# Seven edge tiles of a graph kernel are placed and scattered ahead of the count of all edges

## The chip, the cores and the metric

The kernel runs on one core of one Trainium2 chip. The metric is the time of one execution on the device, in microseconds; the median of three executions of the kernel before is 2573.27 us (2565.25 to 2579.46).

## What is computed

A graph layer with a mixture block and a mixture of experts behind it. There are 3125 nodes with 512 values each and 50000 edges. Cut to what matters here:

```python
edge_dst, edge_src = edge_index[0], edge_index[1]       # "src" and "dst" of the inputs
w   = ssp(edge_attr @ W_f1) @ W_f2 * (ssp(s0 @ W_s1) @ W_s2)
out0 = w1 * x0e * sh0[:, None] + w4 * einsum('eum,em->eu', x1e, sh1) / sqrt(3)
out1 = ...                                               # x0e, x1e are rows x[edge_src]
out  = segment_sum(concat(out0, out1), edge_dst, num_segments=N)
x = x + gnn(layernorm(x), ...) + linear_attention(layernorm(x))
x = x + mixture_of_experts(layernorm(x))
```

The edges arrive sorted by the inputs' `dst`, but the sum runs over the other index, so the kernel sorts the edges itself.

## The kernel before, in words

**Stage 1, up to about 565 us.** The 50000 edges form 391 tiles of 128 edges, in 14 chunks of 28 tiles (`CT = 28`; `ST = 7` tiles make a segment, `GC = 4` segments a chunk). An edge has a record of 48 floats (`rec`): four values of `edge_attr_4` (loaded as `sh`), both node numbers, the place of its node in its group, and 32 hidden values (`ssp` of `edge_attr_32 @ W_f1`). Nodes fall into 25 groups of 125, and each group into two halves, so there are `NU = 50` lists. A list has `PER * P = 1024` fixed slots (`ROOM`); what does not fit goes to overflow tiles. To find the slot of an edge, the kernel needs its rank in its list:

- `hot(c)` (L252): for each chunk a one-hot table of the edges' lists, 128 x 1400 in bf16, built by VectorE; fourteen of them.
- The count of all edges: 56 matmuls (L260), four per chunk, add the tables up per segment into `ps_tot`; VectorE reduces them (`sums`, L267), two small matmuls make the edges before each segment (`ps_c`) and the totals (`ps_n`), and some twenty VectorE steps (L289 to L313) make `starts` out of them.
- `earlier(c)` (L327, L329) makes `seen`, the edges of the tiles before within the segment; `ranked(c, ks)` (L339, L340, L343) adds three matmuls per segment: the edges above in the tile, `seen`, and `starts`. `own_ranks` (L351) picks each edge's rank, `places` (L358 to L375) turns it into the row of `recs`, held in `at_i`. The last instruction of each call of `places` is noted in `found`.
- `spread` (L419, TensorE), `softened` (L427 to L429, ScalarE), `begin` (L403 to L408) and `joined` (L438, VectorE) fill the record; chunks 0 and 1 stay in SBUF, the others are stored in DRAM (`lined`, L446) and fetched again (`recall`, L519).
- `place(n, behind)` (L529) issues the next `n` scatters on GpSimd: one indirect DMA for each tile, from its records to the rows `recs[at_i]`. With `behind` a scatter also waits for a TensorE instruction, so that they are spread over the stage.

Chunk 0 is counted and placed first, on its own. Then `place(12)` and a hand-ordered schedule of turns follow, in which the chunks 1 to 13 and the 25 node tiles (layer norm, turning, keys) are interleaved; two calls `place(3, last)` stand in each turn. Then a loop over node columns (`place(3, last)` and single ones) and a loop over the 25 node tiles that makes the gather tables `rows_d` and `rows_s` (two calls of `place(2, last)` and one of `place(1, last)` per tile, L987, L1002 and L1025 are the matmuls they wait for). `place(2 * T)` issues what is left. A scatter waits for the clearing of the fixed slots (`cleared`, L183), too.

**Stage 2** loads the sorted records `rec<-recs` (L1104), once all scatters have landed, and then gathers rows, weighs and sums them; **stage 3** is the mixture of experts. Neither is touched by the change.

The order of instructions outside the hand-ordered parts is set by the program's order and by `tc.issue_after`, which puts an instruction behind another in its engine's queue. Each engine runs its queue in order. SP's and ACT's queues also issue loads: SP has `to_i`, `of_i`, `w_f`, `ea` and `sh` of chunks 0 and 1, `random_matrix` and the first three `x`; ACT has `b_out`, `W_o0`, `W_o1` and `W_kT` (1 MB), of which `by_random` (L493) makes `r_W_kT` with 32 matmuls before the first turn.

Of the kernel before, what the change touches and what calls it, by code (L numbers as in the profile page):

```python
# [17 lines left out]
P = 128  # L18
EDGES = 50000
TG = 125  # L20
# [31 lines left out]
def gnn_mix_moe_kernel(ctx: ExitStack, tc: tile.TileContext, a: dict, out: bass.AP):  # L52
# [90 lines left out]
    with ExitStack() as c1:  # L143
# [24 lines left out]

        w_f1 = tmp.tile([P, 4, HID], F32, name="w_f1")
# [77 lines left out]
        hots, counts = [], []  # L247
        ps_t = psum.tile([P, ST * NU], F32, name="ps_tot", tag="at")[:NSG]
        for c in range(NC):
            ts = slice(c * CT, (c + 1) * CT)  # L250
            hots.append(
                nc.vector.tensor_tensor(  # L252
                    hot(c).rearrange("p g (i b) -> p g i b", b=NU),
                    in_half_b[:, ts].rearrange("p (g i) -> p g i", i=ST).unsqueeze(3).to_broadcast([P, GC, ST, NU]),
                    lane_b.unsqueeze(1).unsqueeze(1).to_broadcast([P, GC, ST, NU]), op=ALU.is_equal,
                )
            )
            for g in range(c * GC, (c + 1) * GC):
                counts.append(
                    nc.tensor.matmul(  # L260
                        ps_t, only[:, NSG - 1 - g : 2 * NSG - 1 - g],
                        hot(c)[:, g - c * GC, :],
                        start=(g == 0), stop=(g == NSG - 1),
                    )
                )
        sums = tmp.tile([P, NU], F32, name="sums")
        nc.vector.tensor_reduce(sums[:NSG], ps_t.rearrange("g (i b) -> g b i", b=NU), AX.X, ALU.add)  # L267
        ps_c = psum.tile([P, NU], F32, name="ps_c", tag="t", bufs=1)
        nc.tensor.matmul(ps_c, before2[:NSG, :], sums[:NSG], start=True, stop=True)
        ps_n = psum.tile([P, NU], F32, name="ps_n", tag="k", bufs=1)  # L270
        nc.tensor.matmul(ps_n, ones[:NSG, :], sums[:NSG], start=True, stop=True)


        side_i = tmp.tile([P, T], I32, name="side_i")
        nc.vector.tensor_single_scalar(side_i, in_half_i, 1, op=ALU.bitwise_and)
        in_half = tmp.tile([P, T], F32, name="in_half")
        with tc.issue_after(hots[-1].ins):
            nc.vector.tensor_copy(in_half, in_half_i)
        local = tmp.tile([P, T], F32, name="local")
        nc.vector.scalar_tensor_tensor(local, in_half, -TG / 2, to_i, op0=ALU.mult, op1=ALU.add)  # L280
        nc.vector.scalar_tensor_tensor(local, side_i, -0.5, local, op0=ALU.mult, op1=ALU.add)
        far = float((NFIX + OF) * P - ROOM)
        base_ = tmp.tile([P, T], F32, name="base_")
        nc.vector.scalar_tensor_tensor(base_, side_i, -1.0, in_half, op0=ALU.mult, op1=ALU.add)
        nc.vector.tensor_scalar(base_, base_, float(ROOM // 2), far, op0=ALU.mult, op1=ALU.subtract)


        held = srt.tile([P, NG, 2], F32, name="held")
        nc.vector.tensor_copy(held.rearrange("p b h -> p (b h)"), ps_n)  # L289
        many_i = tmp.tile([P, NG, 2], I32, name="many_i")  # L290
        nc.vector.tensor_scalar(many_i, held, float(P - 1 - ROOM), 0.0, op0=ALU.add, op1=ALU.max)
        nc.vector.tensor_single_scalar(many_i, many_i, 7, op=ALU.arith_shift_right)
        many = tmp.tile([P, NG, 2], F32, name="many")
        nc.vector.tensor_copy(many, many_i)
        first = srt.tile([P, 2, NG], F32, name="first")
        for k in range(2):
            nc.vector.tensor_tensor_scan(
                first[:, k, :], ones[:, :NG], many[:, :, k], 0.0, op0=ALU.mult, op1=ALU.add
            )
        nc.vector.tensor_max(pairs_used, first[:, 0, NG - 1 :], first[:, 1, NG - 1 :])  # L300
        nc.vector.tensor_sub(first, first, many.rearrange("p b h -> p h b"))
        over_at = tmp.tile([P, NG, 2], F32, name="over_at")
        nc.vector.tensor_scalar(
            over_at, first.rearrange("p h b -> p b h"), float(-OF), 65536.0, op0=ALU.add, op1=ALU.mult
        )
        base_i = tmp.tile([P, NU], I32, name="base_i")
        nc.vector.tensor_copy(base_i, ps_c)
        nc.vector.tensor_single_scalar(base_i[:LO], base_i[:LO], -256, op=ALU.bitwise_and)
        nc.vector.tensor_single_scalar(base_i[LO:], base_i[LO:], 255, op=ALU.bitwise_and)
        starts = tmp.tile([P, NU], BF16, name="starts")  # L310
        nc.vector.tensor_copy(starts[:LO].rearrange("p (b h) -> p b h", h=2), over_at[:LO])
        nc.vector.tensor_copy(starts[:NSG], base_i[:NSG])
        nc.vector.tensor_copy(starts[LO:], base_i[LO:])  # L313
# [19 lines left out]
        def ranked(c, ks):  # L333

            so = seen[c % 2]
            for k in ks:
                g = c * GC + k
                ps = ranks[k] = psum.tile([P, ST * NU], F32, name="ps_at", tag="at")
                nc.tensor.matmul(ps, after_b, hot(c)[:, k, :], start=True, stop=False)  # L339
                nc.tensor.matmul(  # L340
                    ps[:, NU:], ones_b, so[:, k, 1:, :].rearrange("p i b -> p (i b)"), start=False, stop=False
                )
                nc.tensor.matmul(  # L343
                    ps.rearrange("p (i b) -> p i b", b=NU), part_of[:, g : g + 1].to_broadcast([P, P]),
                    starts.unsqueeze(1).to_broadcast([P, ST, NU]), start=False, stop=True,
                )

        def own_ranks(c, ks):

            for k in ks:  # L350
                nc.vector.tensor_mul(  # L351
                    mine[:, k * ST : (k + 1) * ST, :].rearrange("p i b -> p (i b)"), ranks.pop(k), hot(c)[:, k, :]
                )

        def places(c):

            ts = slice(c * CT, (c + 1) * CT)
            nc.vector.tensor_reduce(slot, mine, AX.X, ALU.add)  # L358
            nc.vector.tensor_copy(slot_i, slot)


            nc.vector.tensor_single_scalar(rank, slot_i, 65535, op=ALU.bitwise_and)
            nc.vector.tensor_single_scalar(which, slot_i, 16, op=ALU.arith_shift_right)
            nc.vector.scalar_tensor_tensor(moved, which, float(P), base_[:, ts], op0=ALU.mult, op1=ALU.subtract)
            nc.vector.scalar_tensor_tensor(moved, rank, float(ROOM), moved, op0=ALU.is_ge, op1=ALU.mult)
            nc.vector.scalar_tensor_tensor(moved, moved, far, base_[:, ts], op0=ALU.add, op1=ALU.add)
            nc.vector.tensor_add(slot_i, moved, rank)

            at = at_i[:, ts]
            nc.vector.tensor_scalar(at, slot_i, P - 1, 2, op0=ALU.bitwise_and, op1=ALU.logical_shift_left)  # L370
            nc.vector.tensor_scalar(which, slot_i, 6, 2, op0=ALU.arith_shift_right, op1=ALU.bitwise_and)
            nc.vector.tensor_tensor(at, at, which, op=ALU.bitwise_or)
            nc.vector.tensor_scalar(which, slot_i, -2 * P, 1, op0=ALU.bitwise_and, op1=ALU.logical_shift_left)
            nc.vector.tensor_tensor(at, at, which, op=ALU.bitwise_or)
# [9 lines left out]
        def edges_of(c):  # L384
# [3 lines left out]
            nc.sync.dma_start(  # L388
                ea, a["edge_attr"][:, c * CT * P : (c + 1) * CT * P].rearrange("f (r e) -> r f e", r=4)
            )  # L390
            sh = mk.tile([P, CT, 4], F32, name="sh")
# [30 lines left out]
        def softened(c, part):  # L422
# [6 lines left out]
            nc.scalar.activation(sp[:, :m], sp[:, :m], AF.Ln, bias=half, scale=0.5)  # L429
            sps[c, part] = ps, sp  # L430

        def joined(c, part):

            ps, sp = sps.pop((c, part))
            i0, i1 = PARTS[part]
            m = i1 - i0
            for r in range(4):
# [9 lines left out]

        edges_of(0)
        edges_of(1)
        with tc.issue_after(hots[-1].ins):  # L450
            begin(0)
        with tc.issue_after(counts[len(counts) // 2].ins):
            for part in range(2):
                spread(0, part)
                softened(0, part)
        earlier(0)
        for ks in ((0, 1), (2, 3)):
            ranked(0, ks)
            own_ranks(0, ks)
        places(0)  # L460
        for part in range(2):
            joined(0, part)
# [3 lines left out]
        def load(name, shape, src, pool=w, tag=None):  # L466
            t_ = pool.tile(shape, F32, name=name, tag=tag or name)
            nc.scalar.dma_start(t_, src)
# [31 lines left out]
        w_rk = by_random("W_kT", wide("W_kT"))  # L500
# [15 lines left out]
        def recall(c):  # L516
            if DIRECT <= c < T // CT:
                again[c] = chk.tile([P, CT, REC], F32, name="again", bufs=2)
                nc.gpsimd.dma_start(again[c], lined[c])  # L519

# [1418 lines left out]
```

## Time and profile before

| what | value |
|---|---|
| median of three executions | 2573.27 us |
| profiled execution | 2575.68 us |
| its span | 2573.9 us |
| PE / DVE / ACT / POOL busy in the span | 91% / 64% / 49% / 59% |
| first to last scatter, L529 | 46.24 to 565.13 us, 391 of them |
| stage 2 and 3 | 565 to 2574 us |

PE is TensorE, PEld its weight loads, DVE is VectorE, ACT is ScalarE, POOL is GpSimd and SP is SyncE; a letter q behind an engine's name marks its queue. A line of the timeline has start, duration, engine, line of the kernel, operation, and the tiles as output <- input; in brackets stands how long the engine was idle before it and what ended that. A line of a table by stretches of time has the stretch, its length, the busy time and number of instructions of PE, PEld, DVE, ACT and POOL (or of the one engine asked for), the granted TensorE clock as a share of full speed, the busy share of the DMA engines and what they moved in GB/s. Busy shares over the whole span say little here, because the stages have different limits: POOL is busy in 59% of the span, but in stage 1 its scatters follow each other nearly without a gap.

### The profile page before, as it was taken

The numbers are of one execution on the slowest core, as the hardware profiler recorded it, in microseconds if no ns is written. First come the engines' busy times: TensorE is split into PE (matmuls) and PEld (weight loads), VectorE is DVE, ScalarE is ACT, GpSimd is POOL, SyncE is SP. The second block draws the span as 40 slices with busy tenths as digits, with TensorE's granted clock in tenths as the row PEclk, the third lists the DMA queues.
The fourth block names the chain that finished last, engine by engine and source line by source line (L and its number), as shares of the span: only waits on it lengthen the run. The fifth ranks groups of instructions, "written<-read, shape, count | busy, mean of one in ns | idle before, by whom it ended". The sixth has DMA issues, their size and how long they took to land. (4 is left out here: it accounts for less than half of the span.)

```text
span 2573.9 us, 46654 instructions
## 1 busy us (share of the span) xinstructions
PE 2347.7 (91%) x16977; PEld 1522.1 (59%) x16977; DVE 1634.8 (64%) x3130; ACT 1254.0 (49%) x3444; POOL 1529.1 (59%) x1488
## 2 busy tenths in 40 slices
PE   6888999408999999999999999984999999999998
PEld 4654456304444444444444444463888888888887
DVE  8887444207999999999999999976222222222222
ACT  2665512105777777777777777752222222222221
POOL 3777767776666666666666666413555555555552
PEclk7999999758999999999999999997999999999999
DMA  4665889528777777777777777545315325857454
GB/s 145 189 209 198 303 294 312 191 65 262 231 229 232 229 230 228 231 229 231 230 228 227 233 228 231 175 164 209 107 51 183 131 56 192 332 186 258 140 171 143
DMA packets 188092, 521.94 MB, mean 203 GB/s; under 512 B 55421, under 2 KB 84166, under 8 KB 177104
## 3 DMA queue, kind: packets, MB, share of 16 engines
q0 software_dynamic: 110224, 397.55, 48.2%
q1 hardware_dynamic: 71296, 115.05, 13.6%
q10 hardware_dynamic: 6336, 6.28, 0.8%
q8 instruction: 137, 2.24, 0.3%
q14 instruction: 99, 0.81, 0.1%
HBM read 586.07 MB, written 104.25 MB: 268 GB/s over the span
## 5 line engine op out<-in xcount | busy, mean ns | idle before, releaser
L1127 POOL DMA_INDIRECT gx<-rows_s,rec x416 | 445.5, 1071 | 326.5 <-DVE ft L1284 217.7
L1304 PE MATMUL ps_s<-ft,ones 128*64 128x256 f32 (+1 forms) x3328 | 493.8, 439 | 10.0 <-DVE acc L1318 9.9
L1250 ACT ACTIVATE ones<-one,rec 128x64 f32<-128x64 f32 x1664 | 429.5, 337 | 0.0
L1800 PE MATMUL ps_f<-h,we 128*128 128x128 f32 x3328 | 394.4, 277 | 1.2 <-DVE h L1815 1.2
L1813 ACT ACTIVATE h<-ps_f,bias 128x128 f32<-128x128 f32 x312 | 114.5, 368 | 575.2 <-PE ps_f L1800 558.7
L529 POOL DMA_INDIRECT recs<-again,at_i x335 | 326.3, 974 | 113.9 <-issue 78.9
L1800 PEld LDWEIGHTS ps_f<-h,we 128*128 128x128 f32 x3328 | 379.8, 192 | 3.1 <-DVE h L1815 1.6
L1284 DVE TENSOR_TENSOR ft<-wt,gx 128x768 f32<-128x768 f32 x416 | 378.3, 951 | 0.0
L1815 DVE TENSOR_SCALAR h<-ps_f,bias 128x128 f32<-128x128 f32 x312 | 108.6, 350 | 422.7 <-PE ps_f L1800 419.0
L1304 PEld LDWEIGHTS ps_s<-ft,ones 128*64 128x64 f32 x3328 | 222.2, 136 | 228.3 <-issue 148.5
L1720 POOL DMA_INDIRECT we<-w_rows,w_at x208 | 211.6, 1017 | 215.4 <-PE ps_y L1832 93.3
L1266 DVE TENSOR_TENSOR wt<-wt,wb 128x1024 f32<-128x1024 f32 x208 | 253.2, 1217 | 59.7 <-ACT wt L1265 59.2
L1123 POOL DMA_INDIRECT gd<-rows_d,rec x208 | 252.6, 1214 | 64.6 <-issue 64.3
L1265 ACT COPY wt<-wa 128x1024 f32<-128x1024 f32 x208 | 211.3, 1016 | 126.2 <-PE wb L1263 126.2
L1262 PE MATMUL wa<-w_f,hT 32*128 32x512 f32 x832 | 236.8, 640 | 0.0
L1263 PE MATMUL wb<-w_s,hT 32*128 32x512 f32 x832 | 235.8, 640 | 0.0
L1800 PEld LDWEIGHTS ps_f<-xt,we 128*128 128x128 f32 x1664 | 195.4, 193 | 25.5 <-issue 23.7
L1800 PE MATMUL ps_f<-xt,we 128*128 128x128 f32 x1664 | 195.8, 276 | 0.7 <-ACT xt L1748 0.7
L1832 PE MATMUL ps_y<-we,h 128*128 128x512 f32 x416 | 192.4, 605 | 0.1
L1182 PEld LDWEIGHTS ps_ip<-ident,prod 128*128 128x128 f32 x1248 | 136.6, 142 | 78.7 <-ACT oneT L1152 77.2
L1182 PE MATMUL ps_ip<-ident,prod 128*128 128x128 f32 x1248 | 161.6, 280 | 0.7 <-ACT oneT L1152 0.7
L1280 DVE TENSOR_TENSOR ft<-wt,gx 128x512 f32<-128x512 f32 x208 | 144.0, 692 | 7.1
(394 smaller groups left out, 3282.2 us busy)
## 6 DMA issues: line engine op xcount, KB each, us to landing
w_rows<-in_Wh SPq DMA_DIRECT2D x24, 1024.0 KB
rows_s<-r SPq DMA_DIRECT2D x24, 448.0 KB
rec<-recs SPq DMA_DIRECT2D x104, 96.0 KB
w_rows<-in_Wo SPq DMA_DIRECT2D x8, 1024.0 KB
lined<-rec SPq DMA_DIRECT2D x12, 672.0 KB
again<-lined POOLq DMA_DIRECT2D x12, 672.0 KB
gx<-rows_s,rec POOLq DMA_INDIRECT x416
xs<-acc POOLq DMA_DIRECT2D x25, 256.0 KB
```

The source lines that it names most:

```text
L529: put = nc.gpsimd.indirect_dma_start(out=recs[:, :], out_offset=bass.IndirectOffsetOnAxis(ap=at_i[:m, t : t + 1], axis=0), in_=again[c][:m ...
L1123: nc.gpsimd.indirect_dma_start(out=Q.gd[:, i - 2, :], out_offset=None, in_=rows_d[:, :], in_offset=bass.IndirectOffsetOnAxis(ap=reci[:, i, ...
L1127: nc.gpsimd.indirect_dma_start(out=Q.gx[:, i, :], out_offset=None, in_=rows_s[:, :], in_offset=bass.IndirectOffsetOnAxis(ap=reci[:, i, 4:5 ...
L1182: nc.tensor.matmul(ps[:, i, :], Q.prod[:, i, b * P : (b + 1) * P], ident, is_transpose=True, start=(b == 0), stop=(b == 2),)
L1250: nc.scalar.activation(R.ones[:, k, c, :], R.Q.one[:, i, :], AF.Copy, scale=R.Q.rec[:, i, c : c + 1])
L1262: nc.tensor.matmul(wa[:, k, :], Q.hT[r, 0, :], w_f2[r, :], start=True, stop=True)
L1263: nc.tensor.matmul(wb[:, k, :], Q.hT[q, 1, :], w_s2[q, :], start=True, stop=True)
L1266: nc.vector.tensor_mul(R.wt, R.wt, wb)
L1284: nc.vector.tensor_mul(R.ft[:, k, MUL : 7 * MUL].rearrange("p (b c u) -> p b c u", b=2, c=3), w[:, k, :, 1, :].unsqueeze(2).to_broadcast([ ...
L1304: nc.tensor.matmul(to, R.ones[:, k, m, :], what, start=(first and m == 0), stop=(last and m == 3), tile_position=(0, k * HT),)
L1720: nc.gpsimd.indirect_dma_start(out=dst, out_offset=None, in_=src, in_offset=bass.IndirectOffsetOnAxis(ap=at[:, j : j + 1], axis=0), bounds ...
L1800: nc.tensor.matmul(pss[f], ws[l][:, k, f * P : (f + 1) * P], h[:, k, :], start=(k == 0), stop=(k == 3))
```

## The change

The first segment of chunk 0, seven tiles with 896 edges, has no edges before it, and no list can hold more than 896 of them, so their ranks need neither `starts` nor a test against the 1024 fixed slots. They are placed, and their scatters issued, before the count of all edges. In the program's order it goes: one-hot of chunk 0; the six helper tables for chunk 0 alone (`numbers`); `seen` of chunk 0; two matmuls for segment 0 (without the third); `own_ranks`, `begin`, `places(0, 0, 7)` with a short form; four more one-hots; `joined` for the tiles of the first segment; `place(7)`; then the other one-hots, the count, the helper tables of the other chunks, and the other three segments of chunk 0.

```diff
         def ranked(c, ks):
             so = seen[c % 2]
+            blind = c == 0 and ks == (0,)
             for k in ks:
...
+                if blind:
+                    return last
                 nc.tensor.matmul(
                     ps.rearrange("p (i b) -> p i b", b=NU), part_of[:, g : g + 1].to_broadcast([P, P]),
...
+        edges_of(0)
+        assert ST * P <= ROOM
+        hots.append(one_hot(0))
+        numbers(slice(0, CT))
+        earlier(0)
+        seg0 = ranked(0, (0,))
+        for part in range(2):
+            with tc.issue_after(seg0.ins):
+                spread(0, part)
+            soft = softened(0, part)
+        with tc.issue_after(own_ranks(0, (0,)).ins):
+            begin(0)
+        places(0, 0, ST)
+        edges_of(1, found[0])
+
+        for c in range(NC):
+            if c:
+                with tc.issue_after(found[0].ins):
+                    hots.append(one_hot(c))
+            if c == 4:
+                with tc.issue_after(hots[-1].ins):
+                    for part in range(2):
+                        joined(0, part, range(1))
+                place(ST)
+            for g in range(c * GC, (c + 1) * GC):
+                counts.append(
...
+        with tc.issue_after(hots[-1].ins):
+            numbers(slice(CT, T))
+        for ks in ((1,), (2, 3)):
+            ranked(0, ks)
+            own_ranks(0, ks)
+        places(0, ST, CT)
+        for part in range(2):
+            joined(0, part, range(1, 4))
+        stored(0)
```

Some loads move as well. `sh` of chunk 0 is issued third on SP, ahead of `w_f`; `ea` and `sh` of chunk 1 and the first three `x` come behind the placing of segment 0 (`found[0]`, by waits); `W_kT` waits for the last step of `softened(0, 1)` on ACT.

```diff
+            came = nc.scalar.dma_start(t_, src)
+            if name == "W_kT":
+                after_it(came, soft)
...
         for t in range(3):
-            x_of(t)
+            after_it(x_of(t), found[0])
         place(12)
```

All later calls of `place` stand where they stood, with the same numbers, so each issues tiles seven further on, and the last call finds seven fewer.

## The prediction

> **What bounds the kernel now.** The page's chain of what ended last holds only the last 30 us of the kernel, so I read stage 1 from tables by stretches and from the timeline. First the stretches around the end of stage 1:
>
> ```profile
> 440.00:480.00 40.00, 40.00 (x175) 26.50 (x174) 18.76 (x47) 10.39 (x26) 30.71 (x33) 1.00 0.92 321
> 480.00:500.00 20.00, 0.91 (x3) 0.01 (x1) 1.52 (x4) 0.37 (x1) 15.28 (x16) 0.64 0.39 125
> 500.00:565.00 65.00, 0.00 (x0) 0.00 (x0) 0.96 (x8) 0.00 (x0) 49.46 (x53) 0.50 0.13 37
> ```
>
> PE is done at about 481; from there to 565 only POOL works. Then POOL's timeline, with the first instructions of stage 2:
>
> ```profile
> 46.24 1.04 POOL L529 DMA_INDIRECT recs<-rec,at_i  x1 [37.97 <-DVE at_i L375]
> 47.59 1.00 POOL L529 DMA_INDIRECT recs<-rec,at_i  x1 [0.31 <-issue]
> ...
> 327.97 0.95 POOL L529 DMA_INDIRECT recs<-again,at_i  x1 [2.30 <-PE ps_p L987]
> 337.09 0.96 POOL L529 DMA_INDIRECT recs<-again,at_i  x1 [6.83 <-PE ps_nn L1002]
> 356.69 0.96 POOL L529 DMA_INDIRECT recs<-again,at_i  x1 [2.19 <-PE ps_p L987]
> 359.99 0.96 POOL L529 DMA_INDIRECT recs<-again,at_i  x1 [1.08 <-PE ps_nn L1002]
> ...
> 564.21 0.92 POOL L529 DMA_INDIRECT recs<-again,at_i  x1 [0.30 <-issue]
> 566.51 48.28 SPq L1104 DMA_DIRECT2D rec<-recs  x9
> 568.56 0.33 DVE L1109 TENSOR_TENSOR rec<-rec,real_slot 128x160 int32<-128x160 int32 x1 [64.91 <-DMA rec<-recs]
> ```
>
> The last scatter releases the load of the records, for which DVE had been idle 64.91 us: the last scatter sets the start of stage 2. Scatters follow each other with 0.30 us between them, with four exceptions at 328 to 360, where POOL has caught up with PE and waits 2.00 + 6.53 + 1.89 + 0.78 = 11.2 us beyond the 0.30. This is the main point: **an earlier start of POOL at 46 us is worth nothing, since it would be waited away at 328 to 360. The end is PE's time at 360, and behind it the scatters that are left, one after the other.**
>
> Last, the front, where the count sits:
>
> ```profile
> 7.85 18.40 DVE L252 TENSOR_TENSOR xT<-in_half_b,lane_b 128x1400 bf16<-128x1400 bf16 x12
> ...
> 29.23 0.35 DVE L278 CAST in_half<-in_half_i 128x392 f32<-128x392 int32 x1
> ...
> 34.69 0.18 DVE L312 CAST starts<-base_i 56x50 bf16<-56x50 int32 x1
> ...
> 37.33 0.98 DVE L351 TENSOR_TENSOR mine<-ps_at,xT 128x350 f32<-128x350 f32 x2
> ...
> 40.07 7.08 PE L493 MATMUL ps_r<-r,W_kT 128*128 128x64 f32 x32
> ...
> 45.77 0.19 DVE L375 TENSOR_TENSOR at_i<-at_i,side_i 128x28 int32<-128x28 int32 x1
> ```
>
> DVE works without a gap up to 38; the 32 matmuls of L493 come behind chunk 0's ranks and hold up what PE does for the turns, with which the rest of stage 1 moves.
>
> **The change part by part.** *Tail.* Every later call of `place` is kept, so behind the wait at 360 there are seven scatters fewer. From 513.61 to 564.21 lie 40 steps, 1.265 us each: 7 x 1.265 = **8.9 us less**. Nothing covers them. The seven themselves move to about 22 to 31 us, where POOL was idle (its 37.97 us), and cost nothing there if they are through before `place(12)`.
>
> *Front: when the one-hots end.* DVE reaches the first one-hot at 7.85 as before. Then, in DVE's new order: one-hot 1.53 (18.40 / 12), to 9.3; `seen` and four 28-wide helpers, 0.2 + 5 x 0.29 (the five adds of the chunk at 57.56 took 1.46) + 4 x 0.1, to 11.4; one matmul and its hand-overs 0.75 (DVE to PE 0.16 and 0.46 for L340 at 36.46, 0.12 back), to 12.2; `own_ranks` 0.5; `begin` 0.65 (as at 60.98 to 61.63); a reduction of 7 of 28 columns, 0.4 out of 1.61; seven dependent small steps, 1.7 (the same chain for chunk 1 took from 55.61 to 57.07, and one step more), to 15.4. Four one-hots 6.1 and two joins 0.4, to 21.9; nine more one-hots 13.8, to **35.7 instead of 29.2: 6.5 us later**. What waits behind this on DVE is the whole count.
>
> *Front: what is given back.* Before, `starts` was complete 5.6 us behind the one-hots, own ranks came at 8.1 because `seen` was made in between, and L493 began at 10.8 (40.05) behind two rounds of ranks. Now `seen`, `begin` and one segment are done. `starts` comes at about 6.0 (the chain of reduction, two matmuls and small steps stays; five joins of some 0.2 and one 0.48 helper replace records and `seen`), the first own ranks at 6.7, and one round (1.25 us, 38.23 to 39.48) instead of two follows: L493 begins at 8.4. Given back: 2.4 us. **PE's stage moves by 6.5 - 2.4 = 4.1 us.** `at_i` of chunk 0's rest comes 3.4 us later, about 49.6; POOL's `place(12)` starts there, which the 11.2 us absorb.
>
> *Does the shift reach 360?* From 60 to 255 turn follows turn with DVE 87% busy (64.93 of 75 us at 75 to 150), and all loads are issued by the same queues: I pass the whole 4.1 on.
>
> *Bounds of the shift.* The records' join now stands in DVE's queue ahead of nine one-hots and waits for `ea`, PE's `spread` and ACT's `softened` (5.8 us, from 21.80 to 27.61). The DMA engines were full until 17.5 before; without `W_kT` and chunk 1's `ea` (1.5 MB of some 5.8 MB issued by 13) they are free at about 14, so the join's data are there at about 20 and the join at 21.5 does not wait. If `ea` only lands at 18, it waits 2.7. So the shift lies between 2.5 (small steps cheaper) and 7. The moved loads cost nothing: `W_kT` is issued at about 21 and needed at 44; the three `x` are issued at 16 to 18 instead of 21.7; `ea` of chunk 1 is needed at about 40. SP has nothing urgent behind its wait for `found[0]`, and behind ACT's wait for `softened` the next instruction is at 42. What covers them is at least 12 us, and a late one would move the turns one for one. Tiles are needed seven scatters earlier: tile 28 at 49.6 + 21 x 1.265 = 76, when chunk 1's records, joined at 64 before, are ready at 68; chunk 2's fetch at 94, stored at 79. Stages 2 and 3 keep their order and move as a whole.
>
> *Sum:* -8.9 + 4.1 = **-4.8 us**: the span goes from 2573.9 to 2569.1. The profiled execution (2575.68 with what lies around its span) stands 2.4 us above the median of 2573.27; on the median the forecast is 2573.27 - 4.8 = **2568.5 us**.
>
> **Two rules against rows.** The clock in the front:
>
> ```profile
> 46.00:47.00 1.00, 1.00 (x7) 0.50 0.00 0
> 47.00:48.00 1.00, 0.86 (x4) 0.50 0.07 23
> 51.00:52.00 1.00, 1.00 (x6) 0.50 0.09 25
> 52.00:53.00 1.00, 1.00 (x10) 0.97 0.03 11
> ```
>
> PE was busy from 36 on, yet the granted clock was 0.50 until 52, behind an idle time from 31.6 to 35.9; the new order has an idle time as long in the same place, so I keep 7.08 us for L493. The Trainium skill, "TensorE: Matmul & The Clock Gate", section "Part 1: The HAM clock gate (the "warmup" mystery)", has the clock come back after one busy window of about 3.4 us; by it L493 could run at twice the speed, some 3.5 us would be saved and the sum would be -8.3; this trace disagrees with it by its sixteen slow microseconds.
>
> DVE and POOL at once: the seven scatters lie under one-hots, which read two tiles from SBUF. The 25 `seen` adds (two SBUF inputs, too) between 57 and 120 us, with scatters running, took 0.264 us in the median against 0.250 for ten between 30 and 44 without, and scatters kept 1.265 us. Fourteen one-hots cost nothing measurable at that rate. The Trainium skill, "SBUF — State Buffer", section "Who interferes with whom", says that a DVE instruction with two SBUF inputs is blocked by a GpSimd instruction that reads SBUF; by it up to 7 x 0.96 = 6.7 us of one-hots would be lost and the sum would be +1.9.
>
> **The rivals.** *A, the joins or the one-hots are held up by the new work* (slower). Place: DVE at 21.5 to 31, where the join and nine one-hots stand behind `ea` and beside the scatters. The seven scatters keep POOL busy 7 x 0.96 = 6.7 us; if DVE lost all of that, the shift would be 10.8 and the median 2573.3 + 1.9 = 2575. It decides from 4.8 us of lost time on; against it stand 0.264 and 0.250. To be slower by 0.5%, 17.7 us would have to be lost, for which no row speaks.
>
> *B, PE's stage does not move.* If the clock is full at L493 (3.5 of 7.08) and the front is 1 us shorter than worked out, the shift is about -0.4, and the whole tail remains: -9.3, 2564. For it: a full clock at 25 to 31 in this trace. Against: sixteen slow microseconds.
>
> *C, it doesn't do what it says.* The seven scatters could be held up by the clearing of `recs` (2.4 MB issued at 1.91) or DVE's order; then POOL starts later, but the wait at 360 absorbs up to 11 us, and the count behind it is still seven fewer. It would give 2568 too, unless the seven run into `place(12)` by more than 11 us, for which clearing would have to last past 50; before, DMA had fallen to 0.33 at 18. So this one gives no other time.
>
> **How the numbers follow.** A median of three runs here spans 2565 to 2579, and less than 0.5%, 13 us, can't be told from no change. Forecast (shift 2.5 to 7, -6.4 to -1.9): 0.72. A: 0.12, B: 0.14, C or something unseen: 0.02. The forecast's own range with some 4 us of the measurement on each side is 2563 to 2575; with A and B, 2559 to 2578. B, and the forecast with an accident of the runs, can pass -13: faster 0.12. A at its full price is still within 0.5%: slower 0.05. Within 0.5%: 0.83.
>
> **What would show it.** Right: the first scatter at 22 to 23 and seven before 32, the eighth at about 50; one-hots ending near 36; L493 at 43 to 45; POOL again waiting for PE at 328 to 365, by a similar sum; the last scatter ending near 560. Wrong: no waits for PE there (then the start of POOL counts), L493 at 40 or at 48, one-hots over 1.6 us beside scatters, the join idle on ACT, or a stage 2 and 3 of other length than 2008.8 us.

## The result and the profile after

The changed kernel takes 2577.81 us in the median of 20 executions (2571.57 to 2587.84), the kernel before, run beside it, 2570.54 us (2564.97 to 2579.46, 20 executions). The ratio is 1.0026, with a 95% interval of 1.0016 to 1.0036: some 7 us more, between 4 and 9, where the prediction had 4.8 us less. The time lies within 0.5% of before and just within the widest range that was stated (2559 to 2578), but outside the forecast's own 2563 to 2575, and the change went the other way.

The profiled execution of after took 2575.23 us, its span is 2573.5 us. First the table by stretches at the end of stage 1, as shown of before:

```profile
440.00:480.00 40.00, 38.39 (x157) 25.17 (x157) 20.90 (x48) 8.16 (x23) 30.43 (x32) 1.00 0.86 275
480.00:500.00 20.00, 10.95 (x57) 7.13 (x55) 5.58 (x16) 3.72 (x9) 15.12 (x17) 0.86 0.71 259
500.00:565.00 65.00, 0.00 (x0) 0.00 (x0) 1.04 (x8) 0.00 (x0) 49.27 (x52) 0.50 0.17 49
```

PE still works for 10.95 us between 480 and 500, where before it worked for 0.91: its part of stage 1 ends some 10 us later. POOL has nearly the same work behind it as before, 52 instructions from 500 on instead of 53. POOL's timeline, with the load that begins stage 2:

```profile
26.56 1.04 POOL L438 DMA_INDIRECT recs<-rec,at_i  x1 [18.22 <-DVE rec L415]
...
36.07 1.23 POOL L438 DMA_INDIRECT recs<-rec,at_i  x1 [0.30 <-issue]
56.12 0.96 POOL L438 DMA_INDIRECT recs<-rec,at_i  x1 [18.83 <-DVE at_i L339]
...
342.81 0.95 POOL L438 DMA_INDIRECT recs<-again,at_i  x1 [6.23 <-PE ps_nn L1053]
362.36 0.96 POOL L438 DMA_INDIRECT recs<-again,at_i  x1 [2.18 <-PE ps_p L1038]
393.30 0.96 POOL L438 DMA_INDIRECT recs<-again,at_i  x1 [2.26 <-PE ps_nn L1053]
...
563.60 0.92 POOL L438 DMA_INDIRECT recs<-again,at_i  x1 [0.30 <-issue]
565.89 3.59 SPq L1155 DMA_DIRECT2D rec<-recs  x7
567.94 0.33 DVE L1160 TENSOR_TENSOR rec<-rec,real_slot 128x160 int32<-128x160 int32 x1 [54.62 <-DMA rec<-recs]
```

The seven scatters are done by 37.3, in what was idle time, and the eighth comes at 56.12. POOL catches up with PE at 343 to 362, as before, but then waits once more at 393, which it didn't before. The last scatter ends at 564.52 (563.60 + 0.92), against 565.13 before. From there to the end of the span are 2009.0 us, against 2008.8: the stages behind did not change. Last the front, from the timelines of DVE and PE:

```profile
14.54 6.19 DVE L456 TENSOR_TENSOR xT<-in_half_b,lane_b 128x1400 bf16<-128x1400 bf16 x4
21.49 3.32 PE L395 MATMUL ps_h<-w_f,ea 128*128 128x128 f32 x14 [9.74 <-DMA ea<-in_edge_attr]
25.98 0.29 DVE L415 SCALAR_TENSOR_TENSOR rec<-ps_h,sp 128x128 f32<-128x128 f32 x1 [5.26 <-ACT sp L405]
27.04 0.26 DVE L415 SCALAR_TENSOR_TENSOR rec<-ps_h,sp 128x96 f32<-128x96 f32 x1 [0.77 <-ACT sp L405]
27.21 10.77 DVE L456 TENSOR_TENSOR xT<-in_half_b,lane_b 128x1400 bf16<-128x1400 bf16 x7
37.90 3.14 DVE L456 TENSOR_TENSOR hot_late<-in_half_b,lane_b 128x1400 bf16<-128x1400 bf16 x2
50.31 3.95 PE L568 MATMUL ps_r<-r,W_kT 128*128 128x64 f32 x32
```

Four one-hots end at 20.7. Then DVE stands for 5.26 and 0.77 us before the two joins, because ScalarE's `softened` isn't there, because PE's `spread` began only at 21.49, because it waited for `ea` of chunk 0. The other nine one-hots stand behind these joins and end at 41.0 instead of 29.3, and the 32 matmuls of `by_random` begin at 50.31 instead of 40.07.

### The profile page after: what moved, and what is told of

It reads as the page before. It is cut to its first block, busy times and chain, and to the rows that moved or that the text cites. A ratio compares the mean times of both kernels' runs of the same rounds, so it can differ in the third digit from the quotient of the medians.

```text
span 2573.5 us, 46667 instructions
## 1 busy us (share of the span) xinstructions
PE 2344.1 (91%) x16976; PEld 1520.0 (59%) x16976; DVE 1637.8 (64%) x3144; ACT 1253.8 (49%) x3444; POOL 1529.2 (59%) x1488
```

## The experiments

All of them compute the whole output. "Loop" is the time from the first to the last `ps_nn` matmul of the loop over the 25 node tiles; the expectations count to the start of the last group of them, some 1.5 us less (147.4 for 149.0). Profiles of one kernel differ, so before and after were profiled twice:

| kernel | time, us | ratio to before, 95% | `by_random` begins, lasts | loop, us | last scatter ends |
|---|---|---|---|---|---|
| before | 2570.54 | | 40.07, 7.08 | 149.0 | 565.13 |
| e5_before_again | 2576.76 (one) | | 39.97, 4.41 | 147.0 | 563.69 |
| after | 2577.81 | 1.0026 (1.0016 to 1.0036) | 50.31, 3.95 | 153.2 | 564.52 |
| e4_after_again | 2577.36 | 1.0011 (0.9991 to 1.0031) | 49.26, 6.92 | 154.8 | 568.36 |
| e1_place19 | 2567.27 | 0.9982 (0.9966 to 0.9999) | 40.38, 3.81 | 153.8 | 559.69 |
| e2_join_late | 2571.59 | 0.9997 (0.9979 to 1.0016) | 43.29, 3.79 | 154.8 | 559.46 |
| e3_ea_16 | 2573.99 | 0.9996 (0.9979 to 1.0013) | 44.83, 6.93 | 152.4 | 563.42 |
| e6_loads_back | 2596.37 | 1.0073 (1.0048 to 1.0098) | 64.20, 6.93 | 153.2 | 582.59 |
| e7_unbound | 2574.16 | 0.9986 (0.9971 to 1.0002) | 40.48, 4.34 | 157.4 | 560.28 |
| e8_both | 2565.60 | 0.9957 (0.9941 to 0.9973) | 45.76, 6.93 | 152.4 | 555.20 |

Each group of runs has its own runs of before beside it (2570 to 2577 us in the median), so the ratios are what compares.

### The tail alone: seven scatters more in the call ahead of the turns

```diff
-        place(12)
+        place(19)
```

This is the kernel before with nothing of the new front. 

> The kernel before, with nineteen instead of twelve scatters free of any wait for TensorE, and nothing else. Theory T (the end of stage 1 is TensorE's stage plus the scatters left behind its last wait): POOL keeps its pace, its waits for TensorE at 328 to 360 us shrink from 11.2 to about 2 us beyond the usual 0.30, seven scatters fewer are left, the last scatter ends 8.9 us earlier, near 556, and the time is about 9 us less than before (0.35%). Rival S (POOL's start sets the end): no change, last scatter at 565.

Measured: 0.9982, and the last scatter 5.4 us earlier than in the first profile of before, 4.0 earlier than in e5_before_again, whose `by_random` is as short as here. Two lines of its POOL timeline:

```profile
389.33 0.96 POOL L529 DMA_INDIRECT recs<-again,at_i  x1 [3.31 <-PE ps_nn L1002]
...
558.77 0.92 POOL L529 DMA_INDIRECT recs<-again,at_i  x1 [0.30 <-issue]
```

Seven scatters fewer in the bound calls are worth something without any new front, though 4.0 to 5.4 and not 8.9 us. The waits at 328 to 360 shrink to 2.7 us beyond the 0.30, as expected; much of the rest is lost in waits such as the one at 389.33, in the middle of a node loop that is 4.8 us longer than in the first profile of before.

### The join behind all one-hots

```diff
-            if c == 4:
-                with tc.issue_after(hots[-1].ins):
-                    for part in range(2):
-                        joined(0, part, range(1))
-                place(ST)
...
+        with tc.issue_after(hots[-1].ins):
+            for part in range(2):
+                joined(0, part, range(1))
+        place(ST)
```

From the changed kernel: the two joins no longer stand in front of nine one-hots. 

> The changed kernel, with the join and the seven scatters behind all fourteen one-hots instead of behind the fifth. Theory J (the join holds up VectorE, because the edge attributes land at 21.5 us): the 6.0 us of idle time go, the one-hots end near 35 instead of 41, L568 starts near 44 instead of 50, and the time is 6 us less than the changed kernel's, about that of before. Rival K (the loss lies in what is given back behind the count, or in later stages): the one-hots end earlier, but the time stays within 2 us of the changed kernel's.

```profile
35.02 1.31 POOL L438 DMA_INDIRECT recs<-rec,at_i  x1 [26.61 <-DVE rec L415]
...
43.08 0.96 POOL L438 DMA_INDIRECT recs<-rec,at_i  x1 [0.30 <-issue]
49.09 0.96 POOL L438 DMA_INDIRECT recs<-rec,at_i  x1 [5.05 <-DVE at_i L339]
...
558.54 0.92 POOL L438 DMA_INDIRECT recs<-again,at_i  x1 [0.30 <-issue]
```

The one-hots end at 34.5 instead of 41.0, `by_random` begins at 43.29 instead of 50.31, and the last scatter ends at 559.46 instead of 564.52. The scatters come 8.5 us later than in the changed kernel and lose nothing by it: they are still through before the eighth. The joins' place costs some 5 us at the end of stage 1, and 5.8 us by the medians (2571.59 against 2577.36, run beside each other; 3.6 by the ratios, whose intervals overlap). About 6 were expected.

### The load of `ea` on more DMA engines

The table by stretches of the changed kernel, while `ea` comes:

```profile
14.00:16.00 2.00, 0.00 (x0) 0.00 (x0) 1.90 (x5) 0.00 (x0) 0.00 (x0) 1.00 0.25 96
16.00:18.00 2.00, 0.00 (x0) 0.00 (x0) 2.00 (x3) 0.00 (x0) 0.00 (x0) 1.00 0.66 195
18.00:20.00 2.00, 0.00 (x0) 0.00 (x0) 2.00 (x2) 0.00 (x0) 0.00 (x0) 1.00 0.66 132
20.00:22.00 2.00, 0.51 (x2) 0.54 (x3) 0.72 (x1) 0.00 (x0) 0.00 (x0) 1.00 0.27 93
```

A DMA share of 0.25 to 0.27 at some 95 GB/s, at 14 to 16 and at 20 to 22, is what 4 of 16 engines would show with 12 of them idle. The load's pattern (`"f (r e) -> r f e"`) has 4 as its outermost dimension. The Trainium skill, "DMA: Bandwidth & Descriptors", section "Why a DMA increments its semaphore by 16 and not by 1", says that the number of engines is the largest, 16 at most, that divides the outermost dimension of both sides of a transfer; the other side here is the 128 partitions of `ea`, and the row agrees. So the edit splits it, from the changed kernel:

```diff
+            if c == 0:
+                n = CT // 4 * P
+                for r in range(4):
+                    came = nc.sync.dma_start(
+                        ea[r * HID : (r + 1) * HID, :], a["edge_attr"][:, c * CT * P + r * n : c * CT * P + (r + 1) * n]
+                    )
+            else:
...
```

> The changed kernel, with chunk 0's edge attributes loaded by four transfers of 32 partitions each instead of one whose outermost dimension is 4. Theory Q (that load moves at a quarter of the DMA engines: share 0.25 to 0.27 and about 100 GB/s while nothing else runs): the first matmul on them starts at 12 to 15 us instead of 21.5, the join at 21 does not wait, and the time is 6 us less than the changed kernel's. Rival (the load is late because it is queued behind the clearing): it starts at 18 or later and the time falls by less than 3 us.

```profile
14.00:16.00 2.00, 0.00 (x0) 0.00 (x0) 1.90 (x5) 0.00 (x0) 0.00 (x0) 1.00 0.58 175
```

```profile
16.92 3.16 PE L402 MATMUL ps_h<-w_f,ea 128*128 128x128 f32 x14 [5.02 <-DMA r<-in_random_matrix]
...
44.83 6.93 PE L575 MATMUL ps_r<-r,W_kT 128*128 128x64 f32 x32
```

The DMA share at 14 to 16 is 0.58 instead of 0.25 (the table by stretches), and `spread` begins 4.6 us earlier (PE's timeline). That is later than the 12 to 15 us that were expected, and the profile puts the end of this wait down to the load of `random_matrix`, so `ea` may have been there before. The first scatter comes at 21.86 instead of 26.56, the one-hots end at 36.3, and the last scatter ends at 563.42. That is 4.9 us earlier than in e4_after_again, which has the same slow `by_random`; its three lines, from the timelines of DVE, PE and POOL:

```profile
25.72 0.29 DVE L415 SCALAR_TENSOR_TENSOR rec<-ps_h,sp 128x128 f32<-128x128 f32 x1 [5.19 <-ACT sp L405]
49.26 6.92 PE L568 MATMUL ps_r<-r,W_kT 128*128 128x64 f32 x32
567.45 0.91 POOL L438 DMA_INDIRECT recs<-again,at_i  x1 [0.30 <-issue]
```

With the data there, the front comes out close to the prediction: first scatter 22 to 23, one-hots 35.7, `by_random` 44.2 were forecast (40.07 + 4.1). The time is 3.4 us below the changed kernel's by the medians (2573.99 against 2577.36; the intervals of the ratios overlap), of 6 expected.

### Both kernels again

> The changed kernel again, for a second profile and a time beside the others on this chip. If the first profile is typical, the join waits 6 us again, the one-hots end near 41 and TensorE's node loop ends 8 to 10 us later than before (489.7 against 479.7). If the first profile was a lucky one (L568 took 3.95 us at full clock against 7.08), L568 takes about 7 us and the last scatter ends at 567 to 570. The time should be 6 to 7 us above the kernel before.

> The kernel before once more, for a second profile. In its first profile TensorE's node loop took 147.4 us from the first to the last ps_nn group (330.74 to 478.16); in the five profiles with seven scatters placed earlier it took 151.0 to 153.3. Theory L (the loop is slowed by the scatters, which are seven further on): 147 to 148 again, and no waits of POOL for TensorE behind 360. Rival (chance, as the transfers of that loop fall): 150 to 153, waits at 385 to 425 too, and a last scatter near 565 to 569 all the same.

In e4 DVE waits 5.19 and 0.77 us before the joins again, and the time is 2.9 us above before by the medians, where 6 to 7 were expected. What differs between the two profiles of one kernel is `by_random`: 3.95 and 6.92 us for the same 32 matmuls in after, 7.08 and 4.41 in before. The granted clock differs with it, as two rows of the tables by stretches show, after and then e4:

```profile
51.00:54.00 3.00, 3.00 (x30) 3.00 (x28) 2.97 (x14) 1.59 (x3) 0.00 (x0) 1.00 0.00 0
50.00:56.00 6.00, 6.00 (x30) 6.00 (x30) 5.14 (x32) 1.53 (x3) 0.94 (x1) 0.50 0.00 0
```

PE is busy throughout in both; its clock is full in one and half in the other. Why is not settled by any run. In after the last scatter ends at 564.52 and 568.36. In before the ends of `by_random` lie 2.8 us apart, but POOL's wait at 356.69 comes at 356.55 in e5, and the last scatter 1.4 us earlier. e5's loop is no longer than before's, and POOL has no wait over 0.4 us behind 360, as was expected if the scatters' place lengthens the loop. So the pair of profiles in the section on the result sets a long `by_random` of before beside a short one of after; by like pairs the last scatter is 0.8 us later (564.52 against 563.69) or 3.2 us later (568.36 against 565.13), and all four pairs span -0.6 to +4.7.

### The waits of the moved loads

The changed kernel without the waits of `W_kT`, of `ea` and `sh` of chunk 1 and of the first three `x`:

```diff
-        edges_of(1, found[0])
+        edges_of(1)
...
-            if name == "W_kT":
-                after_it(came, soft)
...
-            after_it(x_of(t), found[0])
+            x_of(t)
```

> The changed kernel without the waits of the loads: W_kT, chunk 1's edge attributes and sh, and the three x are issued as early as before. Theory Q (chunk 0's edge attributes use a quarter of the DMA engines, behind whatever is queued there): they land later, the join waits 8 us or more instead of 6.0, the time is 2 to 4 us above the changed kernel's. Rival (the waits of the loads cost time themselves, for the first turns): L568 starts no later, and the time is 2 us or more below the changed kernel's.

```profile
29.98 0.69 DVE L604 BATCH_NORM_STATS2 bn<-x 128x6 f32<-128x512 f32 x1 [19.73 <-DMA x<-in_x]
31.79 0.41 PE L299 MATMUL ps_at<-seen,ones_b 128*128 128x300 bf16 x1 [20.41 <-DVE seen L287]
32.00 3.33 PE L395 MATMUL ps_h<-w_f,ea 128*128 128x128 f32 x14
41.66 2.32 POOL L438 DMA_INDIRECT recs<-rec,at_i  x1 [33.16 <-DVE rec L415]
```

The front is lost: `spread` begins at 32.00 instead of 21.49, and the first scatter comes at 41.66. But it is not lost in the way that was expected. `spread` has no wait for `ea` here; it stands behind the matmul of segment 0's ranks, which waits 20.41 us for `seen`, and DVE, whose queue now has a node tile's statistics in the middle of `seen`, waits 19.73 us for `x`. The time is 0.48 to 0.98% over before, some 12 to 16 us above the changed kernel by the ratios, where 2 to 4 were expected. So the waits are no ornament of the change: without them, work that needs a late load stands ahead of segment 0's ranks in DVE's queue. What the earlier loads cost `ea` can't be read from this run.

### Fewer bindings

Six calls between the turns and the node loop (two each in `sums_turned`, `values` and `values_out`) take one scatter each. On top of e1, and then on top of e3:

```diff
-            place(1, last)
+            place(2, last)
```

```diff
-            place(1, last)
+            place(3, last)
```

> The kernel before with nineteen free scatters and six more in the column loop (two instead of one beside the six matrix steps of the mixture block). Theory T (TensorE's stage plus what is left behind the last wait): the 7 us of waits that the run with nineteen still had between 330 and 420 go to below 2, six scatters fewer are left, the last scatter ends 5 to 7 us before that run's 559.7, at 553 to 555, and the time is about 10 us less than before (0.4%). Rival: the waits only move on in the node loop, and the time is that of the run with nineteen.

> The changed kernel with chunk 0's edge attributes on all DMA engines, and twelve more scatters in the column loop (three instead of one at each matrix step). Theory T: its 14 us of waits for TensorE shrink below 3, the last scatter ends 11 to 13 us before the run without them (563.4), at 550 to 553, and the time is 11 to 13 us below that run's, about 11 below the kernel before. If the seven early scatters are worth anything, it is here: it should end before the run e7. Rival: POOL's start does not matter at all, and it ends no earlier than e7.

```profile
474.04 0.96 POOL L445 DMA_INDIRECT recs<-again,at_i  x1 [1.29 <-DVE r L1066]
...
554.29 0.91 POOL L445 DMA_INDIRECT recs<-again,at_i  x1 [0.30 <-issue]
```

In e7 the six scatters bring no further gain: the last one ends at 560.28, 0.6 us after that of e1. POOL's waits for PE behind 310 are gone, as expected, but there is one idle time of 5.86 us ahead of 473.66 that the profile puts down to nothing; without it the last scatter would end near 554.7 by my estimate (560.28 - 5.56), where 553 to 555 was expected. In e8 twelve more scatters are issued before the node loop, POOL waits just once behind 310, 1.29 us, and the last scatter ends at 555.20, 9.9 us earlier than before (550 to 553 was expected) and 5.1 earlier than in e7. With 0.9957 it beats both kernels. How much of that the early scatters bring is not shown, since no run has twelve more scatters without the new front.

### The recalls' place

Why is the node loop longer where the scatters run seven ahead? The recalls of stored records (672 KB each, on POOL's queue) then fall seven scatters earlier, among the node tiles' loads. So they were issued seven scatters later with the scatters ahead (e9, e11 on e1; e16, e17 on after) and seven earlier without (e10, e12, e14):

```diff
-                if i == CT // 2:
+                if i == CT // 2 + ST:
```

> The kernel of e1_place19 (before, with seven scatters more at place(12)), but each recall of a chunk's records (672 KB, on POOL's queue) is issued seven scatters later, so at the time at which it was issued before. Theory P (the node loop is longer in every kernel whose scatters run seven ahead because the recalls then fall together with the node loads, y<-out): PE's ps_nn loop takes 145 to 148 us again instead of 152.2, no wait of POOL for PE behind 380, the last scatter ends at 554 to 557 instead of 559.7. Rival L (the loop is longer because the scatters themselves run closer behind PE and their DMA writes or POOL's issue slow the loads; the recall's place doesn't matter): loop 150 to 153 us, POOL waits at 389 again, last scatter at 559 to 561. Rival N (the loop's length varies from profile to profile by 5 us): anything between, with no order.

> The kernel before with each recall issued seven scatters earlier and nothing else. Theory P: the node loop grows from 145 to 147 us to 150 to 153, POOL waits for PE behind 380, last scatter at 567 to 570, time 2 to 6 us over before. Rival L: loop 145 to 148, no such waits, last scatter at 563 to 566, time within 2 us of before. Rival N: a loop between these.

> The kernel of e9_recall_later again, since there the kernel before itself took 2795 us, so that its stage 1 can't be set beside the others'. Theory P (recalls that fall seven scatters earlier collide with the node loads): ps_nn loop 145 to 148 us instead of 152.2 in e1_place19, no wait of POOL for PE behind 380, last scatter at 554 to 557. Rival L (the scatters' own closeness): loop 150 to 153, waits near 389 stay, last scatter at 559 to 561. Rival N (the loop varies by itself): between these, with no order.

> The kernel of e10_recall_earlier again, for the same reason. Theory P: loop 150 to 153 us instead of 145 to 147, POOL waits for PE behind 380, last scatter at 567 to 570, time 2 to 6 us over before. Rival L: loop 145 to 148, no such waits, last scatter at 563 to 566, within 2 us of before. Rival N: between these.

> The kernel before, once more, as the first of four of one call (chunks recalled as before, at tile 14 of the chunk ahead). All theories: ps_nn loop 145 to 148 us if the memory is as fast as in the first runs (about 2575 us of time); if this call meets the slow memory of e11 and e12 (2755 us), some 180 to 190 us. The other three are read against this one.

> The kernel before, recalls seven scatters earlier. Theory P (the recall's phase against the node loads lengthens the node loop): loop 4 to 6 us longer than in e13_before_2x2, last scatter 2 to 5 us later. Rival L (the phase doesn't matter): loop and last scatter within 2 us of e13_before_2x2.

> The changed kernel, once more. Theory P and rival L alike: loop 4 to 6 us longer than in e13_before_2x2, last scatter within 3 us of it, time 0 to 7 us over. Rival N (the loop's length in the first runs was a chance of the profiles): loop within 2 us of e13_before_2x2, last scatter by the 8.9 less the shift of PE's stage, whatever that is here.

> The changed kernel, recalls seven scatters later, so at the time at which they are issued before. Theory P: loop 4 to 6 us shorter than in e15_after_2x2, POOL's waits behind 380 gone, last scatter 4 to 6 us earlier, time 3 to 6 us less. Rival L: loop, waits and last scatter as in e15_after_2x2 within 2 us.

> The changed kernel with recalls seven scatters later, where before has them, on a chip whose memory is as fast as in the first runs (if the kernel before takes some 2575 us; at 2755 or more this tells only what e16 told). Theory P (the recall's phase lengthens the node loop): loop 145 to 148 us instead of 151.8 and 153.3 in the two profiles of the changed kernel, no wait of POOL for PE of over 1 us behind 380, last scatter at 558 to 562. Rival L (the phase doesn't matter): loop 151 to 154, waits behind 380, last scatter 564 to 568.

> The kernel of e8_both once more, to see what is left of its 11 us if the memory is slow (the kernel before at some 2790 us) and the node loop waits for its loads. Theory: stage 1 then ends with PE and not with POOL's queue, so earlier scatters are worth less: ratio 0.997 to 1.001, POOL waiting for PE in sum over 100 us. Rival: the gain is that of the bindings, and stays: ratio below 0.997. If the memory is as fast as in the first runs, the ratio is 0.9941 to 0.9973 again.

These ten runs came to five other chips, on which the kernel before takes 2755 to 2800 us in the median. There PE, DVE and ACT stand still together, as from 57 to 66 in the profile of e13_before_2x2, the kernel before itself (timelines of DVE, ACT and PE):

```profile
65.70 0.42 DVE L617 TENSOR_SCALAR fm<-ps_k 128x256 f32<-128x256 f32 x1 [8.65 <-remote]
67.90 0.59 ACT L603 COPY xT<-ps_t 128x512 f32<-128x512 f32 x1 [9.95 <-remote]
68.54 0.45 PE L339 MATMUL ps_at<-xT,after_b 128*128 128x350 bf16 x1 [12.56 <-ACT xT L603]
```

The idle times of DVE and ACT end with "remote", a releaser that the waits of before and after do not have. I called it slower memory in the expectations; the runs do not show that: the DMA engines move nothing at 66 to 68 either, and where they are full, at 8 to 14, they move 295 to 339 GB/s in e13 and 298 to 351 in the profile of before.

| kernel | ratio to its before, 95% | loop, us | last scatter ends |
|---|---|---|---|
| e13 before | 0.9996 (0.9955 to 1.0038) | 185.6 | 643.69 |
| e14, e10, e12 before, early recalls | 0.9988, 1.0014, 0.9986 | 189.6, 192.7, 192.7 | 636.14, 634.79, 633.29 |
| e15 after | 0.9995 (0.9953 to 1.0037) | 185.7 | 637.30 |
| e16, e17 after, late recalls | 0.9978, 1.0005 | 182.3, 174.5 | 638.58, 645.72 |
| e9, e11 e1, late recalls | 1.0014, 1.0002 | 178.6, 194.1 | 639.07, 642.72 |
| e18 as e8 | 0.9983 (0.9953 to 1.0013) | 197.1 | 630.27 |

All ten intervals hold 1. Only e14 and e16 ran on the chip of e13 and e15. Early recalls go with long loops, as the theory wants (189.6 in e14 against 185.6 in e13), but with early last scatters, which it excludes; late ones go with loops of 174 to 194 us, and the kernel before and the changed one have the same loop there. Among stalls of 3 to 15 us a difference of 5 us isn't told, so this stays open. What these chips do show is that the front repeats: `by_random` begins at 40.05 in e13 and at 50.21 in e15, the 10.2 us of the first pair again. And e8's gain of 11 us isn't confirmed there: its ratio lies in the 0.997 to 1.001 expected if stage 1 ends with PE, but its interval reaches below that, and POOL waits for PE some 60 us in sum instead of over 100.

## Why the prediction was wrong

**What bounds the kernel: right.** The last scatter sets the start of stage 2, and stages 2 and 3 take 2009.0 us against 2008.8. POOL catches up with PE at 343 to 362, where 328 to 365 was said, and waits 7.8 us there beyond the 0.30 instead of 11.2.

**The front up to the ranks of segment 0: right.** The one-hots go on at 14.54, forecast 15.4, and four of them end at 20.7. The seven scatters hide in POOL's idle time, as costed at nothing, though the first comes some four microseconds later than said.

**The step that failed: "PE's stage moves by 6.5 - 2.4 = 4.1 us".** It moved by 10.2 at `by_random` (50.31 against 40.07). (The last one-hot of before ends at 29.31, so the 6.5 should have been 6.4.) Of the 6.1 us missing, 6.0 is the joins' stall (5.26 + 0.77). I had set it at nothing because "they are free at about 14", the DMA engines, from which `ea` was to be there at about 20, with 2.7 us as the dearest case. The engines were free at 14 to 16, but `ea` had only 4 of them, and `spread` began at 21.49: the prediction's own sign of being wrong, "the join idle on ACT". At 16 to 20 the moved loads (chunk 1's `ea`, of the same pattern, and the three `x`, issued from 14.6 on) came beside it, at a share of 0.66; what that added was not measured apart. Rows like these were in the trace of before as well:

```profile
18.00:20.00 2.00, 0.75 (x4) 0.42 (x4) 2.00 (x2) 0.00 (x0) 0.00 (x0) 1.00 0.29 104
20.00:22.00 2.00, 0.96 (x5) 0.55 (x5) 2.00 (x3) 0.00 (x0) 0.00 (x0) 0.83 0.26 98
```

I read when the DMA share fell, not how far. e2 takes the joins out of the way and gets 3.2 us of shift, e3 gives `ea` the engines and gets 4.8, on both sides of 4.1. Given back was 1.5 us instead of 2.4 (9.3 us from the last one-hot to `by_random`, 10.8 before).

**"I pass the whole 4.1 on": wrong in detail.** The 10.2 arrive at POOL's wait as 5.7 (362.36 against 356.69), and as 7.3 in e4 (363.98). 3.1 of the difference in the first pair is `by_random`, which took 3.95 us where I kept 7.08; it is one of two values that both kernels show. The end of `by_random` is 7.1 us later (9.0 in e4), and the 1.4 (1.7) that are left were regained by 360, which I had excluded because of a busy DVE. The two profiles of before regain as much: 2.8 us at the end of `by_random` are 0.1 at POOL's wait.

**The tail, "8.9 us less": over-estimated.** From that wait to the end of the last scatter, before takes 208.4 us and after 202.2: 6.3 us less; in e4 4.1 less. So the last scatter moved by 5.7 - 6.3 = -0.6 in the first pair and by 7.3 - 4.1 = +3.2 in e4. Most of what is missing (2.6 and 4.8 us) is in new waits of POOL behind 380: 2.0 us at 393.30 beyond the 0.30, and in e4 3.4 at 397.20 and 1.6 at 424.68 (in the first pair some longer scatters add 0.8):

```profile
397.20 0.96 POOL L438 DMA_INDIRECT recs<-again,at_i  x1 [3.67 <-PE ps_nn L1053]
424.68 0.96 POOL L438 DMA_INDIRECT recs<-again,at_i  x1 [1.94 <-DVE y L1073]
```

It fits that POOL runs seven scatters closer behind PE and that PE's node loop is longer; no run separates the two. The loop in the views of waits, from its first to its last matmul, first before (330.7 to 479.7), then after (336.5 to 489.7), with waiting engine and line, what it waited for, total us, times, longest:

```profile
DVE y L1019 <- DMA y<-out: 32.9, 13, 6.2
DVE r L991 <- DMA rows_s<-r: 4.7, 4, 1.8
DVE y L1019 <- DMA rows_s<-r: 4.5, 1, 4.5
PE ps_nn L1002 <- DVE xg L971: 5.2, 5, 3.0
```

```profile
DVE y L1070 <- DMA y<-out: 34.9, 14, 7.4
DVE r L1042 <- DMA rows_s<-r: 9.9, 5, 3.2
DVE y L1070 <- DMA rows_s<-r: 6.4, 1, 6.4
PE ps_nn L1053 <- DVE xg L1022: 8.4, 4, 3.3
```

PE waits 3.2 us longer for DVE's next table `xg`, most of the 4.2 us by which the loop is longer. DVE waits 9.1 us longer for transfers, 2.0 of them for the rows `y` of the residual sum and 7.1 at the stores into `rows_s`. The loop is 152.4 to 157.4 us in all eight profiles listed with scatters seven or more ahead, 147.0 and 149.0 in the two without; DVE's waits for these two transfers come to 46 to 53 us in the eight and to 41 and 42 in the two, PE's for `xg` to 9 to 13 and to 6. That it goes with the change is shown on these chips, why is not: the recalls' place was tried and not settled, and the scatters' own closeness was not tried.

**What the profiles don't cover.** Like pairs of profiles make 0.8 to 3.2 us of loss (all four pairs -0.6 to 4.7). That fits the second comparison (1.0011, so 2.8 us, from 2.3 less to 8 more), but not quite the first, 4 to 9. The median of before itself was 2570.54, 2574.48 and 2577.16 in three groups of runs, that of after 2577.81 and 2577.36 in two. So the sign is measured in the first comparison, and a loss of some 3 us is accounted for; the rest of the first 7 is not.

**The rules.** `by_random` by the clock rule would be half as long: it was in after, e1 and e2 and not in e3, e4 and e8, and both values come up in before and in after, with a granted clock of 1.00 or 0.50, so neither my 7.08 nor the rule holds alone. The contention of DVE and POOL: the one-hots under the scatters took 1.54 us (10.77 / 7) against 1.55 (6.19 / 4) without, but the scatters there came 1.53 us apart instead of 1.265. DVE loses nothing; POOL gives way, with time to spare. The Trainium skill, "SBUF — State Buffer", section "Who interferes with whom", says that the two contend and that the order of issue decides which one is held; the prediction priced only the case in which DVE is.

**The rivals.** A is the case that came nearest: "the join and nine one-hots stand behind `ea`" was its place, 4.8 us of lost time its point of decision, and 6.0 were lost, but by its first half, the load, and not by contention with the scatters that set its price. B did not come, since PE's stage moved; C neither.

## What to carry to other kernels

Before a consumer is moved ahead of other work in an in-order queue, ask when its farthest input lands, and read the DMA share while that input alone is moving: 0.25 means that the transfer has a quarter of the engines while the others stand idle, so that freeing more of them is not what it needs. If work is to leave the end of a queue, first try to issue more of it in a place that already exists (`place(19)` instead of `place(12)`, 0.9982) before building it a new front that everything else must wait behind. When an effect of 0.3% is at stake, profile each kernel twice: here the same 32 matmuls took 3.8 to 4.4 or 6.9 to 7.1 us, whatever the kernel, and the last scatter of one kernel ended 1.4 us (before) or 3.8 us (after) apart.

## What was unexpected in the hardware

- The 32 matmuls `ps_r` take about 4 or about 7 us from run to run of one kernel (3.95 and 6.92 in after, 7.08 and 4.41 in before), at a granted clock of 1.00 in the short one of after and of 0.50 in the long ones, with PE busy in all of them.
- Beside one-hots the scatters' pitch grows from 1.265 to 1.53 us, about one one-hot (POOL's busy part 1.22 instead of 0.96), and the one-hots stay at 1.54.
- A load with 4 as its outermost dimension moved at some 95 GB/s and a DMA share of 0.25, with nothing else in the way; as four loads it let its first matmul begin 4.6 us earlier.
- On five other chips the same kernel before takes 7 to 9% longer, with PE, DVE and ACT idle together for up to some 10 us.
